# A state-space layer and a soft mixture of experts on one core: TensorE's due sums move between the halves of its long pieces

## The chip, the cores and the metric

The program runs on one NeuronCore of one Trainium2 chip. The metric is the time of one execution on the device in microseconds (us); the lower the better. TensorE is called PE here, VectorE DVE, ScalarE ACT, GpSimd POOL and SyncE SP, as in the profile.

## The reference, cut to what matters

The input x has 16 sequences of 512 positions and 256 channels. First comes a bidirectional state-space layer: a projection to 512 inner channels, a causal convolution of width 4, then for each of two directions, each of the 512 channels and each of 16 states a running sum over the positions:

```
dA_cum = exp(reverse cumulative sum of dt * A[d, n])
xs     = cumsum(dt * u * B[n] * dA_cum) / (dA_cum + 1e-12)
y      = sum over n of xs[n] * C[n]  +  u * D
```

The result is gated and projected back to 256 channels, and `x = layernorm(x + layer(x))`. Then comes a soft mixture of 16 experts with 64 slots each over groups of 1024 positions (two sequences):

```
logits   = layernorm(x) . slot embeddings          (1024 positions x 1024 slots)
slots    = softmax over positions (logits)^T . x   (dispatch)
eout     = (gelu(slots Wg + bg) * (slots Wu + bu)) Wd + bd,  for each expert
out      = softmax over slots (logits) . eout      (combine)
```

and again `x = layernorm(x + experts(x))`. All data are float32.

## The kernel before

A sequence is called a batch b in the code (b = 0 to 15). For each batch `scan_part` runs four times: two directions r and two halves p of the channels, a half having two chunks c of 128 channels. It loops over pairs of states n and over the two chunks, so there are 8 x 2 steps in a part and 1024 steps in all. One step does this:

- ACT makes two exponentials `h` (L420) and two tanh `th` (L422);
- POOL makes `db` = dt*u*B for the two states (L403);
- DVE runs two scans (L426 forward, L428 backward) and two products `hg` (L431); the tile `hg` has four buffers (`bufs=4`);
- POOL multiplies `hg` by C for both states (L432);
- PE sums `hg` over the states into a PSUM tile `acc` by eight transposes (L347). This is the sum that the change moves. For the first states of a part a term u*D follows (L360), and at the very first a matmul with zeros opens the tile (L343).

The sum isn't issued in the step that makes its product. The step appends it to `pending`, and `add_up(depth)` issues the oldest sums until no more than `depth` are left; the step calls `add_up(2)` as the last thing, so a sum is issued two steps after its product was. In states 5 and 13 the product with B is made by PE instead of POOL (`by_diagonal`, tile `hd`, L381), at the step's start.

All other work is cut into pieces and given out beside the scan. A piece is the code of a generator between two `yield`s, and there are three queues of generators (class `Side`): `prep` for the projections of the next part, `front` for the end of a batch (`finish`, `dispatch`) and `back` for experts and combine. `beside_scan` takes up what was left open (evictions of PSUM by ACT or DVE, after `yield HOLD`) and then gives out at most one piece of each queue. Two pieces lie in a step where their turn and the number of free PSUM banks (three, `bank`) allow it. The end of a step reads:

```
                    beside_scan()
                    if k == 1:
                        diags.pop(0)
                    add_up(2)
```

In PE's order a step is therefore: `hd` where there is one, a piece of `prep`, of `front`, of `back`, and the sum.

The pieces of `back` are these. For each pair of experts: both gate matmuls `pg` (L801 for the bias, L806), both up-projections `pu` (L755, function `up`), both down-projections into one bank `peo` (L782, function `down`). ACT evicts `pg` by Gelu into `ht` (L823 the first, L826 the second), DVE multiplies `ht` by `pu` (L767) and makes `eo` of `peo` (L843). For each 128 positions of combine: both halves of the logits `cl` (L860), evicted by DVE's maxima (L868, L869) and ACT's exponentials `cm` (L874), then transposes `ctp` (L881) and the product with the experts' outputs `cpo` (L938). `front` has transposes `pyt` (L598), the output projection `po` (L609, added to x by DVE at L618), dispatch logits `pl` (L663, evicted by DVE's maximum `nm` at L668 and ACT's `et` at L674 and L676), transposes `pd` (L680, evicted to `dis` at L685) and slots `pq` (L695, evicted to `sl` at L705). `prep` has `pin`, `pres`, `px`, `pz` and `pdu`, among them DVE's `rr` (L313).

The experts of two batches are a group. Group g runs beside the scans of batch 2g + 3 (and 2g + 4 has the combines), so the first experts start with batch 3. The eighth group runs after the last scan, from 5160 us on, with wider buffers.

Weights are loaded by SP (`prefetch`, L736) into three buffers (tag `W`), in the order gate, gate, up, up, down, down. SP also loads B and C of each step (L392, L393).

A framework puts the traced instructions into each engine's queue. `late(...)` pins an instruction behind everything traced before it on its engine; `add_up` does so with the first transpose of a sum.

Of the kernel before, what the change touches and what calls it, by code (L numbers as in the profile page):

```python
# [53 lines left out]
def seq_layers(tc, ident, neghalf, a, out):  # L54
# [22 lines left out]
    with ExitStack() as ctx:  # L77
# [27 lines left out]
        def bank(name):  # L105
            count[0] += 1
            if tail and count[0] % 8 >= 3:
                return tail[0].tile([P, 512], F32, tag="tps", name=name)
            return ps.tile([P, 512], F32, tag="mps", name=name)
# [54 lines left out]
        def late(ins):  # L164

            return tc.keep_in_program_order(ins)
# [549 lines left out]
        def experts(g, lo, hi):  # L716

            b0, rows = 2 * g, 2 * SL
            needs = []
            for ep in range(lo, hi):  # L720
                e0 = 2 * ep
                needs += [("Wg", e0), ("Wg", e0 + 1)]
                needs += [("Wu", e0), ("Wu", e0 + 1), ("Wd", e0), ("Wd", e0 + 1)]
            got, used = {}, [0]

            def prefetch():
                while len(got) < min(used[0] + (AHEAD if wide else 3), len(needs)):
                    key, e = needs[len(got)]
                    if wide:
                        t = wide[0].tile([P, 4 * DM], F32, tag="tW", name=f"{key}_{g}_{e}", bufs=AHEAD)  # L730
                    else:
                        t = p2.tile([P, 4 * DM], F32, tag="W", name=f"{key}_{g}_{e}", bufs=3)
                    src = a[key][e]
                    k = src.shape[0] // P
                    t = t.rearrange("p (k f) -> p k f", k=k)
                    nc.sync.dma_start(t, src.rearrange("(k p) f -> p k f", p=P))  # L736
                    got[key, e] = t

            def load_slots(ep):
                st = p1.tile([P, NM, 2, 2 * SL], F32, tag="st", name=f"st_{g}_{ep}")  # L740
                for k in range(NM):
                    nc.sync.dma_start(
                        st[:, k, :, :],
                        s_dram[b0 : b0 + 2, k, :, ep * 2 * SL : (ep + 1) * 2 * SL].rearrange("b p s -> p b s"),
                    )
                return st

            prefetch()
            st = load_slots(lo)
            yield 0  # L750
            def up(e, j, st):
                pu = bank(f"pu_{g}_{e}")
                for fc in range(NF):
                    for k in range(NM):
                        nc.tensor.matmul(  # L755
                            pu[:, fc * P : (fc + 1) * P],
                            got["Wu", e][:, k, fc * P : (fc + 1) * P],
                            st[:, k, :, j * SL : (j + 1) * SL],
                            start=(k == 0),
                            stop=(k == NM - 1),  # L760
                        )
                used[0] += 1
                return pu

            def times(e, ht, pu):
                for fc in range(NF):
                    ins = nc.vector.scalar_tensor_tensor(  # L767
                        ht[:, fc, :],
                        pu[:, fc * P : (fc + 1) * P],
                        biases["bu"][:, e * NF + fc : e * NF + fc + 1],  # L770
                        ht[:, fc, :],
                        ALU.add,
                        ALU.mult,
                    )
                    if fc == 0:
                        late(ins)

            def down(e0, hts):
                po = bank(f"peo_{g}_{e0}")
                for j, ht in enumerate(hts):  # L780
                    for fc in range(NF):
                        nc.tensor.matmul(  # L782
                            po[:, j * DM : (j + 1) * DM],
                            ht[:, fc, :],
                            got["Wd", e0 + j][:, fc, :],
                            start=(fc == 0),
                            stop=(fc == NF - 1),
                        )
                used[0] += 2
                return po  # L790

            for ep in range(lo, hi):
                e0 = 2 * ep
                yield 2
                pgs = []
                for j in range(2):
                    e = e0 + j
                    pg = bank(f"pg_{g}_{e}")

                    own = ident[: NE * NF, e * NF : (e + 1) * NF].unsqueeze(2).to_broadcast([NE * NF, NF, P])  # L800
                    nc.tensor.matmul(  # L801
                        pg.rearrange("p (f s) -> p f s", f=NF), biases["bg"], own, start=True, stop=False
                    )
                    for fc in range(NF):
                        for k in range(NM):
                            nc.tensor.matmul(  # L806
                                pg[:, fc * P : (fc + 1) * P],
                                got["Wg", e][:, k, fc * P : (fc + 1) * P],
                                st[:, k, :, j * SL : (j + 1) * SL],
                                start=False,  # L810
                                stop=(fc == NF - 1 and k == NM - 1),
                            )
                    pgs.append(pg)
                used[0] += 2
                yield HOLD
                prefetch()
                hts = []
                for j, pg in enumerate(pgs):
                    e = e0 + j
                    ht = p2.tile([P, NF, rows], F32, tag="ht", name=f"ht_{g}_{e}")  # L820
                    args = (ht.rearrange("p f s -> p (f s)"), pg, AF.Gelu)
                    if j == 0:
                        late(nc.scalar.activation(*args))  # L823
                    else:
                        with tc.high_priority():
                            nc.scalar.activation(*args)  # L826
                    hts.append(ht)
                yield GAP + 2
                pus = [up(e0 + j, j, st) for j in range(2)]
                if ep + 1 < hi:  # L830
                    st = load_slots(ep + 1)
                bd = p2.tile([P, 2, DM], F32, tag="bd", name=f"bd_{g}_{e0}", bufs=1)
                nc.sync.dma_start(bd, a["bd"][e0 : e0 + 2, :].unsqueeze(0).to_broadcast([P, 2, DM]))
                yield HOLD
                prefetch()
                for j in range(2):
                    times(e0 + j, hts[j], pus[j])
                yield GAP + 1
                po = down(e0, hts)
                yield HOLD  # L840
                prefetch()
                eo = p2.tile([P, 2, DM], F32, tag="eo", name=f"eo_{g}_{e0}", bufs=1)
                late(nc.vector.tensor_tensor(eo.rearrange("p e o -> p (e o)"), po, bd.rearrange("p e o -> p (e o)"), ALU.add))  # L843
                nc.sync.dma_start(e_dram[e0 : e0 + 2, b0 * SL : (b0 + 2) * SL, :].rearrange("e s o -> s e o"), eo)
# [6 lines left out]
        def weights(b, lc, x2, keep):  # L851
# [3 lines left out]
            t = x2.pop()  # L855
            cls = []
            for h in range(2):
                cl = bank(f"cl_{i}_{h}")
                for k in range(NM):
                    nc.tensor.matmul(  # L860
                        cl, t[:, k, :], seT[:, k, h * 512 : (h + 1) * 512], start=(k == 0), stop=(k == NM - 1)
                    )
                cls.append(cl)
# [34 lines left out]
        def all_weights(b, kept):  # L898
            x2 = [load_x2(b, 0)]
            yield 0  # L900
            for lc in range(NL):
                kept[b, lc] = yield from weights(b, lc, x2, True)
# [111 lines left out]
        back.add(1, all_weights(2 * g, kept))  # L1014
        side_by_side()
        front.add(1, experts(g, 0, 8))
        back.add(1, all_weights(2 * g + 1, kept))
        side_by_side()
# [49 lines left out]
```

## Time and profile before

| | before |
|---|---|
| median of 3 runs | 5432.52 us (5432.14 to 5433.58) |
| the profiled execution, its own time | 5434.84 us |
| its span, first to last instruction | 5432.9 us |
| mean granted clock of TensorE | 0.89 of full speed |
| instructions in the span | 73685 |
| data moved by DMA | 907.73 MB, 167 GB/s on the mean |

A row of a group gives line, engine, operation, what is written and read, the shapes and the number of instructions, then the busy time and the mean of one in ns, then the time that the engine sat idle just before these instructions and what ended most of that. The waits give for each line the instruction that it waited for, the total in us, how often and the longest. Float32 matmuls that aren't transposes show as two records each. PEld stands for TensorE's weight loads, which overlap its matmuls.

### The profile page before, as it was taken

What the parts mean: (1) busy time and instruction counts of PE and PEld (TensorE: products, weight loads), DVE (VectorE), ACT (ScalarE), POOL (GpSimd) and SP (SyncE); (2) the same over time, 40 slices, a digit from 0 to 9 for tenths busy, and PEclk for the clock granted to TensorE, in tenths of its full rate; (3) what the DMA queues carried; (4) which work ended last, traced back from release to release, by engine and by line L of the source; (5) the groups of instructions that cost most, each with busy time, mean ns of one, the idle gap of its engine ahead of it and who ended that gap; (6) DMA issues with size and microseconds to landing.
All of it is one profiled execution on the core that took longest, in us unless ns stands there. A gap on an engine that the chain in (4) does not pass through costs nothing. (4 is left out here: it accounts for less than half of the span.)

```text
span 5432.9 us, 73685 instructions
## 1 busy us (share of the span) xinstructions
PE 4336.3 (80%) x24145; PEld 3393.4 (62%) x24145; DVE 4552.0 (84%) x6276; ACT 4091.6 (75%) x6517; POOL 4732.3 (87%) x2537
## 2 busy tenths in 40 slices
PE   4656666898878977788788978889777887878889
PEld 3545555676667765677656766667656775667657
DVE  6888989889888898888988988988989889887722
ACT  6677777887788777887878887788778887777641
POOL 6999999999999899998999989998999989988600
PEclk7677878898889989899889988899888998989999
DMA  4333434575446754566446754467444774457435
GB/s 129 130 122 132 130 124 131 192 231 161 151 141 212 228 148 145 157 220 213 134 137 195 230 173 150 130 215 231 151 145 143 226 224 132 144 178 234 126 104 184
DMA packets 595237, 907.73 MB, mean 167 GB/s; under 512 B 78083, under 2 KB 384899, under 8 KB 594853
## 3 DMA queue, kind: packets, MB, share of 16 engines
q1 hardware_dynamic: 521156, 859.87, 49.9%
q10 hardware_dynamic: 73696, 43.14, 2.8%
q8 instruction: 192, 3.15, 0.2%
q14 instruction: 193, 1.57, 0.1%
HBM read 840.86 MB, written 62.01 MB: 166 GB/s over the span
## 5 line engine op out<-in xcount | busy, mean ns | idle before, releaser
L432 POOL TENSOR_TENSOR hg<-hg,cs 128x1024 f32<-128x1024 f32 x1024 | 2415.3, 2362 | 129.7 <-DVE hg L431 111.4
L403 POOL TENSOR_TENSOR db<-du,bs 128x1024 f32<-128x1024 f32 (+1 forms) x1024 | 2138.8, 2092 | 240.4 <-DVE h L426 93.5
L347 PE MATMUL acc<-ident,hg 128*128 128x128 f32 x8192 | 1191.7, 296 | 207.3 <-POOL hg L432 183.2
L431 DVE SCALAR_TENSOR_TENSOR hg<-th,h 128x512 f32<-128x512 f32 x1792 | 1186.2, 678 | 188.8 <-PE acc L347 110.4
L347 PEld LDWEIGHTS acc<-ident,hg 128*128 128x128 f32 x8192 | 1053.5, 155 | 399.4 <-POOL hg L432 251.0
L426 DVE TENSOR_TENSOR_SCAN h<-h,db 128x512 f32<-128x512 f32 x896 | 1071.3, 1218 | 97.5 <-ACT h L420 92.0
L428 DVE TENSOR_TENSOR_SCAN h<-h,db 128x512 f32<-128x512 f32 x896 | 1072.1, 1218 | 96.1 <-ACT h L420 92.9
L422 ACT ACTIVATE th<-rr,Ah_f 128x512 f32<-128x512 f32 x1024 | 724.5, 714 | 189.2 <-DVE hg L431 187.7
L422 ACT ACTIVATE th<-rr,Ah_b 128x512 f32<-128x512 f32 x1024 | 721.6, 712 | 166.1 <-DVE hg L431 151.3
L420 ACT ACTIVATE h<-dt,A_f 128x512 f32<-128x512 f32 x896 | 608.0, 681 | 115.2 <-DVE hg L431 112.1
L420 ACT ACTIVATE h<-dt,A_b 128x512 f32<-128x512 f32 x896 | 608.6, 681 | 105.0 <-DVE hg L431 102.9
L663 PE MATMUL pl<-x2T,seT 128*128 128x512 f32 x512 | 286.0, 687 | 73.6 <-DVE hg L431 36.2
L381 PE MATMUL hd<-dg,duT 128*128 128x128 f32 x2048 | 309.0, 300 | 35.3 <-ACT yt L603 15.2
L806 PEld LDWEIGHTS pg<-st,Wg 128*128 128x128 f32 x2048 | 245.4, 196 | 107.8 <-issue 85.4
L381 PEld LDWEIGHTS hd<-dg,duT 128*128 128x128 f32 x2048 | 286.1, 216 | 41.8 <-ACT yt L603 17.8
L938 PE MATMUL cpo<-ceo,ct 128*128 128x256 f32 x1024 | 266.3, 420 | 48.5 <-DVE rr L313 38.8
L782 PE MATMUL peo<-Wd,ht 128*128 128x256 f32 x1024 | 253.5, 403 | 48.2 <-DVE rr L313 30.5
L755 PE MATMUL pu<-st,Wu 128*128 128x128 f32 x2048 | 252.3, 282 | 44.6 <-DMA Wu<-in_Wu_dram 18.6
L755 PEld LDWEIGHTS pu<-st,Wu 128*128 128x128 f32 x2048 | 242.6, 196 | 55.8 <-DVE h L428 17.6
L938 PEld LDWEIGHTS cpo<-ceo,ct 128*128 128x128 f32 x1024 | 214.0, 213 | 99.6 <-DVE rr L313 44.0
L806 PE MATMUL pg<-st,Wg 128*128 128x128 f32 x2048 | 270.3, 287 | 5.6 <-DMA Wg<-in_Wg_dram 3.6
L860 PE MATMUL cl<-seT,cx 128*128 128x512 f32 x512 | 251.3, 631 | 29.1 <-ACT et L674 18.2
(151 smaller groups left out, 6621.3 us busy)
## 6 DMA issues: line engine op xcount, KB each, us to landing
cs<-bc SPq DMA_DIRECT2D x512, 512.0 KB, 4.0
bs<-bc SPq DMA_DIRECT2D x384, 512.0 KB, 5.0
Wg<-in_Wg_dram SPq DMA_DIRECT2D x128, 512.0 KB, 6.1
Wu<-in_Wu_dram SPq DMA_DIRECT2D x128, 512.0 KB, 5.7
Wd<-in_Wd_dram SPq DMA_DIRECT2D x128, 512.0 KB, 5.5
dg<-diag_dram SPq DMA_DIRECT2D x128, 256.0 KB, 4.4
bs<-bc SPq DMA_DIRECT2D x128, 256.0 KB, 3.6
x<-in_x_dram SPq DMA_DIRECT2D x32, 512.0 KB, 6.6
```

What stands on the lines that cost most here:

```text
L347: ins = nc.tensor.matmul(accs[c][:, s], hc[:, j, s], ident, is_transpose=True, start=False, stop=(last and j == 1 and lc == NL - 1),)
L381: ins = nc.tensor.matmul(h[:, s], v[c][3][:, s], dg[:, s], start=True, stop=True)
L403: nc.gpsimd.tensor_tensor(db[:, :k, :], du.unsqueeze(1).to_broadcast([P, k, L]), bs[:, :k, :], ALU.mult)
L420: nc.scalar.activation(hs[j][1], dt, AF.Exp, scale=w["A"][:, c, s])
L422: nc.scalar.activation(ths[j], rr, AF.Tanh, bias=LN_1E12 / 2, scale=w["Ah"][:, c, s])
L426: nc.vector.tensor_tensor_scan(h, dec, add, 0.0, ALU.mult, ALU.add)
L428: nc.vector.tensor_tensor_scan(h[:, ::-1], dec[:, ::-1], add[:, ::-1], 0.0, ALU.mult, ALU.add)
L431: nc.vector.scalar_tensor_tensor(hg[:, j, :], th, 1.0, h, ALU.add, ALU.mult)
L432: nc.gpsimd.tensor_tensor(hg, hg, cs, ALU.mult)
L755: nc.tensor.matmul(pu[:, fc * P : (fc + 1) * P], got["Wu", e][:, k, fc * P : (fc + 1) * P], st[:, k, :, j * SL : (j + 1) * SL], start=(k = ...
L806: nc.tensor.matmul(pg[:, fc * P : (fc + 1) * P], got["Wg", e][:, k, fc * P : (fc + 1) * P], st[:, k, :, j * SL : (j + 1) * SL], start=Fals ...
L938: nc.tensor.matmul(po[:, :DM], cts[sc // 4][:, sc % 4 * P : (sc % 4 + 1) * P], eos[sc // 4][:, sc % 4, :], start=(sc == 0), stop=(sc == NS ...
```

## The change

A call of `add_up(2)` is put between the two halves of the long pieces that have two halves: between the gate matmuls of a pair, between the up-projections, between the two halves of the down-projection, and between the two halves of the combine logits. The call at the end of each step stays.

```
             def down(e0, hts):
                 po = bank(f"peo_{g}_{e0}")
                 for j, ht in enumerate(hts):
+                    if j:
+                        add_up(2)
                     for fc in range(NF):
                         nc.tensor.matmul(
...
                 pgs = []
                 for j in range(2):
+                    if j:
+                        add_up(2)
                     e = e0 + j
                     pg = bank(f"pg_{g}_{e}")
...
                 yield GAP + 2
-                pus = [up(e0 + j, j, st) for j in range(2)]
+                pus = [up(e0, 0, st)]
+                add_up(2)
+                pus.append(up(e0 + 1, 1, st))
                 if ep + 1 < hi:
                     st = load_slots(ep + 1)
...
             for h in range(2):
+                if h:
+                    add_up(2)
                 cl = bank(f"cl_{i}_{h}")
                 for k in range(NM):
                     nc.tensor.matmul(
```

More of the change, by code (lines that the diff above doesn't have):

```diff
@@ L780, in down @@
                 for j, ht in enumerate(hts):
+                    if j:
+                        add_up(2)
                     for fc in range(NF):
@@ L796, in experts @@
                 for j in range(2):
+                    if j:
+                        add_up(2)
                     e = e0 + j
@@ L828, in experts @@
                 yield GAP + 2
-                pus = [up(e0 + j, j, st) for j in range(2)]
+                pus = [up(e0, 0, st)]
+                add_up(2)
+                pus.append(up(e0 + 1, 1, st))
                 if ep + 1 < hi:
@@ L857, in weights @@
             for h in range(2):
+                if h:
+                    add_up(2)
                 cl = bank(f"cl_{i}_{h}")
```

## Prediction

> **What bounds the kernel now.** I read the page first (busy time, groups), then who waited for whom, then the timeline around the places that the change touches.
>
> ```profile
> PE 4336.3 (80%) x24145; PEld 3393.4 (62%) x24145; DVE 4552.0 (84%) x6276; ACT 4091.6 (75%) x6517; POOL 4732.3 (87%) x2537
> ...
> L432 POOL TENSOR_TENSOR hg<-hg,cs 128x1024 f32<-128x1024 f32 x1024 | 2415.3, 2362 | 129.7 <-DVE hg L431 111.4
> L347 PE MATMUL acc<-ident,hg 128*128 128x128 f32 x8192 | 1191.7, 296 | 207.3 <-POOL hg L432 183.2
> ```
>
> POOL is the busiest, but only the stretch before expert work starts runs at its pace: from 300 to 900 us POOL is busy 582 of 600 us. Between 900 and 4800 us POOL is busy 3612 of 3900 us, VectorE (DVE) 3461, TensorE (PE) 3218, ScalarE (ACT) 3121. No engine is full; the time is set by a chain that hops between all four. The change acts there, so what counts is where that chain passes through PE.
>
> ```profile
> DVE hg L431 <- PE acc L347: 110.4, 82, 4.8
> DVE hd L428 <- PE hd L381: 74.0, 48, 9.0
> DVE nm L668 <- PE pl L663: 62.0, 37, 9.2
> DVE ht L767 <- PE pu L755: 56.8, 18, 12.7
> DVE eo L843 <- PE peo L782: 49.0, 19, 5.3
> ```
>
> (Total us, times, longest.) The first row is what the change aims at: DVE wants to write a state product into one of four `hg` buffers, and the sum that reads it (PE, L347) isn't done. The other rows are the counterweight: DVE waits for PE's pieces too, and whatever is put ahead of the end of a piece makes these longer.
>
> **What the Trainium skill says.** "PSUM — Partial Sum Buffer", section "Engine vs sequencer instructions": matmuls start and complete in program order, and the other engines' queues are strict FIFO. So a sum put before a second half delays that half by its whole length, and the reader's engine stands. The trace agrees: in each step PE's records come piece, then sum. "TensorE: Matmul & The Clock Gate", section "What's actually happening": after an idle window TensorE's clock is halved until it was busy again for some us. The trace agrees: half an up-projection takes 1.95 us within a run and 3.75 us after 3.98 us of idleness, and the sum behind it 1.92 instead of 1.04 us.
>
> **The change, part by part.** It adds and removes no instruction and no DMA. `pending` holds three sums at most while pieces are given out, so each inserted `add_up(2)` can give out one sum at most, and the one at the step's end then does nothing. In the last part (after 5160 us) `pending` is empty. Matched against the order on PE, 221 of 1024 sums move: 56 each behind first gates, ups and downs, 53 behind first combine logits. Of each step only the order on PE changes: half, sum, half instead of half, half, sum.
>
> *Wait added.* PE's second half now stands behind the wait of the sum for POOL's product (L432). In all 221 places that product ended before the first half did, by 0.4 us or more. Cost nothing, cover: those 0.4 us; bounds 0 and +5 us.
>
> *Price of a move.* 8 transposes, 1.04 us from first start to last end, 1.0 us net on a running PE, since records overlap (1.9 us for 13 sums with the direct term L360 or a slow clock). The sum ends earlier by the second half and whatever lay between (2 to 3 us), the second half ends 1.0 us later, and PE's work behind both is where it was, unless PE idled before the second half (buffer or DMA wait). That is so in 39 places, and the sum goes into the idle time: 36.6 us in all, most of it off the chain.
>
> *Queues moved past.* None on SP or POOL. The weight buffer of a second half is freed 1.0 us later and its next load (5.5 to 6.1 us to landing) starts later. The one such wait that recurs on the chain, `Wu` at 2362, is issued when SP gets past a `cs` load that waits for POOL, so I take 0; bounds 0 and +1 us for each of 7 expert groups.
>
> *Gains by the naive count.* 49 of DVE's waits on a sum, 61.7 us, are behind sums that move. But look at what ends the next wait:
>
> ```profile
> 2460.53 1.04 PE L347 MATMUL acc<-ident,hg 128*128 128x128 f32 x8
> ...
> 2461.41 1.06 PE L381 MATMUL hd<-dg,duT 128*128 128x128 f32 x8
> 2461.61 0.69 DVE L431 SCALAR_TENSOR_TENSOR hg<-th,h 128x512 f32<-128x512 f32 x1 [1.72 <-PE acc L347]
> ...
> 2462.50 1.23 DVE L426 TENSOR_TENSOR_SCAN hd<-dec,hd 128x512 f32<-128x512 f32 x1 [0.20 <-PE hd L381]
> ```
>
> Start, duration, and in brackets the idle time and its releaser. With the sum before the second gate the 1.72 us go, but the next scan needs `hd`, which PE delivers at 2462.46 in either order, so its 0.20 become 1.9 us. PE works without a gap from 2442 to 2472, so an exchange inside that run helps nobody who waits for the run's later products. The same holds for the waits of 2.3 us at 2304 (then DVE stands for `po`, L618) and at 2527 (then for ACT, next line).
>
> *Losses.* The same kind of place seen from the other side:
>
> ```profile
> 2378.04 0.69 DVE L843 TENSOR_TENSOR eo<-peo,bd 128x512 f32<-128x512 f32 x1
> ...
> 2432.76 0.69 DVE L668 TENSOR_REDUCE nm<-pl 128x1 f32<-128x512 f32 x1 [0.40 <-PE pl L663]
> 2433.49 0.69 ACT L674 ACTIVATE et<-pl,nm 128x512 f32<-128x512 f32 x1 [2.56 <-DVE nm L668]
> ...
> 2526.91 1.04 PE L347 MATMUL acc<-ident,hg 128*128 128x128 f32 x8
> 2527.11 0.60 ACT L826 ACTIVATE ht<-pg 128x512 f32<-128x512 f32 x1 [0.30 <-PE pg L806]
> 2527.72 1.28 ACT L420 ACT_TABLE_LOAD   x1
> ```
>
> The second gate's Gelu (L826) starts 0.04 us after the gate ends (2527.07), and ACT's table load and the exponentials that DVE wants stand behind it: +1.0 us. So does the down-projection's `eo` (2378.04, 0.03 us after `peo` ends), and `nm` of the dispatch logits `pl`, which lie between a second half and the sum, with `et` waiting behind it.
>
> *The sum.* The page's own chain starts at 5084 us, so I followed it on by the same rule, by hand, from 5160 back to 60 us: where an instruction was preceded by idleness, go to its releaser, else to the one before it on its engine. The pattern repeats from expert group to expert group (batches 3, 5, ..., 15). Where the chain leaves PE:
> - for `eo` 11 times, one of them behind a 2.50 us DMA wait that takes the sum in: 10 x 1.0;
> - for the second Gelu 6 times: 6.0; for `nm` behind a delayed `pl` 6 times: 6.0; for slots `pq` behind a second gate once: 1.0;
> - in batch 15 three sums with 0.18 us waits, whose DVE predecessor (`eo`, `nm`) gets late: 2.6. Together +25.6 us.
> - For a sum that moves with a real wait: 6 times, behind the second up-projection that waits for `Wu` (0.51, 0.97, 1.19, 1.04, 0.57, 0.65): -4.9 us. There the sum goes into the DMA wait.
> - 6 times a sum that lay behind `pd` on the chain is now before the second up-projection: -0.4 each, -2.4. Three more sums in DMA or buffer waits of batch 15: -2.4. Together -9.7 us.
> - 4 times for combine logits `cl`, each behind a 3.36 us buffer wait that takes the sum in: 0.
>
> Net +15.9 us. A delay on the chain adds in full; a gain lasts only until the next chain takes over, so the true number is hardly below that by this route, unless the order of the other engines changes. The profiled execution has 5434.84 us (span 5432.9 and 1.9 around it), so 5450.7; the median shown is 2.3 us lower, so **5448 us**.
>
> **Rivals.**
> - *Freed buffers decide (faster).* If DVE keeps what it gains because PE, relieved in 39 places, runs ahead of its consumers, the 61.7 us go and the 31 second halves whose readers already stand waiting cost 1.0 us each: -31, 5402 us. For it: POOL waits 111.4 us for DVE's `hg`. Against: the `hd` wait above. It decides where more than half of the 49 waits aren't followed by another wait for PE within some 5 us; of the 7 in the group from 2255 to 2560 us I found 2 like that.
> - *Exchange without effect.* PE's unbroken runs take in both the gains and the losses: within 10 us of 5432. For it: total work and order of products at the end of a run are the same. Against: the Gelu and `eo` readers have no slack.
> - *Other order elsewhere.* Only some instructions are pinned to program order; the build may place others on DVE or ACT anew once sums sit elsewhere. Up to 30 us either way; nothing in the trace prices it.
> - *No change at all:* were `pending` at two, nothing would move. The order on PE (one sum at the end of every step) excludes that.
>
> **Numbers.** A measurement of this kernel tells about 0.2% (10.9 us) from no change. Forecast 55% (45 slower, 10 within), its own range 5438 to 5464; freed buffers 27% (25 faster, 2 within); no effect 18% (14 within, 2 each side). Faster 0.27, same 0.26, slower 0.47. The range 5410 to 5464 leaves out about 14% below (the stronger half of the freed buffers) and 6% above (bounds of the weight loads, another order).
>
> **What would show it.** Right: the row DVE `hg` on PE `acc` falls from 110 to some 55 us, while `eo` on `peo`, `ht` L826 on `pg` and `nm` on `pl` rise, each by 10 us or more in the scan, and `hd` on PE `hd` rises by 15 or more; POOL's waits for DVE don't fall. Wrong: `hd` doesn't rise and POOL's `hg <- DVE hg` falls by 20 us or more (freed buffers), or the order on DVE and ACT differs.

## The result, and the profile after

| | before | after |
|---|---|---|
| median | 5432.33 us (4 runs, 5424.75 to 5433.58) | 5481.24 us (4 runs, 5479.35 to 5493.22) |
| the profiled execution, its own time | 5434.84 us | 5493.22 us |
| its span | 5432.9 us | 5491.3 us |
| mean granted clock of TensorE | 0.89 | 0.88 |

The ratio is 1.0096 [1.0081, 1.0111]: 49 us slower at the medians. The forecast was 5448 us, 16 us slower; the loss is three times that. The profiled execution after is 12 us above its median, so a few us of its rows are its own. From the page of the kernel after, the busy times and POOL's largest group:

```profile
PE 4380.7 (80%) x24143; PEld 3422.0 (62%) x24145; DVE 4544.9 (83%) x6276; ACT 4141.5 (75%) x6549; POOL 4734.5 (86%) x2537
...
L432 POOL TENSOR_TENSOR hg<-hg,cs 128x1024 f32<-128x1024 f32 x1024 | 2418.4, 2365 | 142.5 <-DVE hg L431 107.3
```

The striking number is ACT's count: 6549 instructions where there were 6517, and 50 us more busy time. The edit touches no ACT instruction. The waits of the kernel after (total us, times, longest):

```profile
DVE h L428 <- ACT h L420: 128.9, 74, 7.0
DVE h L426 <- ACT h L420: 115.3, 53, 7.8
...
DVE hg L431 <- PE acc L347: 83.4, 44, 6.4
...
DVE eo L849 <- PE peo L784: 55.3, 15, 6.3
...
DVE nm L668 <- PE pl L663: 54.0, 27, 9.3
```

DVE's wait for the sums falls by 27 us (110.4 to 83.4). The waits that were to rise by 10 us or more don't: `eo` +6, `nm` -8, ACT's wait for the second gate -4 (23.9 to 19.6). POOL's wait for DVE stays, as forecast (111.4 to 107.3). DVE's waits for ACT's exponentials `h`, which the prediction's list of rows doesn't have, rise from 184.9 us (92.9 and 92.0) to 244.2. So much of the lost time shows as waiting for ACT. Its groups say what the 32 instructions are; the first block is of the kernel before, the second of the kernel after (lines below L780 are shifted there: L823, L826 are L827, L830).

```profile
L420 ACT ACT_TABLE_LOAD x121 | 155.2, 1283 | 2.2
...
L826 ACT ACT_TABLE_LOAD x23 | 29.5, 1283 | 0.4
```

```profile
L420 ACT ACT_TABLE_LOAD x132 | 169.4, 1283 | 2.2
...
L830 ACT ACT_TABLE_LOAD x42 | 53.9, 1283 | 0.7
```

Gelu and the exponential need different tables of function values, and where one follows the other on ACT, a table load (ACT_TABLE_LOAD) stands between them. It is put down to the line of the instruction that needs it. Before, 41 of the 64 second Gelus (L826) found their table still in place, because the first Gelu (L823) stood right ahead of them or only a tanh lay between; after, only 22 do. In 19 more pairs an exponential now stands between the two Gelus. In 13 of them that makes two loads more, for the second Gelu and for the next exponential; in the six that are the last pair of a group it makes one more, as the function behind (L296) needed a load before too. By lines it is +19 at L830, +11 at L420, +7 at L674 and -5 at L422: +32 loads of 1.283 us, 41 us of the 50. The trace agrees with the Trainium skill, "ScalarE: Activation LUTs", section "What ACT_TABLE_LOAD costs", on the load itself (some 1283 ns); the drain of some 1380 ns that the page adds to it does not show here, as the timeline below has no gap around a load.

Where do the exponentials come from? Compared instruction by instruction, PE's queue differs by the moved sums alone (called the exchange from here on), but the framework also placed 1382 of ACT's 6073 instructions, 1954 of DVE's 6276, 145 of POOL's and 388 of SP's in other places than before. The prediction had this as a rival ("other order elsewhere") and left it at 30 us either way.

### The profile page after: what moved, and what is told of

Its sections match the earlier page's. It is cut to its first block, busy times and chain, and to the rows that moved or that the text cites. A ratio compares the mean times of both kernels' runs of the same rounds, so it can differ in the third digit from the quotient of the medians.

```text
span 5491.3 us, 73662 instructions
## 1 busy us (share of the span) xinstructions
PE 4380.7 (80%) x24143; PEld 3422.0 (62%) x24145; DVE 4544.9 (83%) x6276; ACT 4141.5 (75%) x6549; POOL 4734.5 (86%) x2537
## 4 chain that ended last, share of the span: by engine, by line
DVE 36%; PE 23%; ACT 19%; issue 11%; POOL 5%; DMA 2%; DVEq 0%; SPq 0%; ACTq 0%; POOLq 0%
DVE h L428 9%; DVE h L426 9%; DVE hg L431 8%; PE acc L347 4%; ACT h L420 4%; ACT th L422 4%; POOL hg L432 2%; POOL db L403 2%; PE cpo L946 2%; ACT L420 2%; PE pq L695 2%; PE pg L810 2%; PE pl L663 2%; PE hd L381 1%; PE peo L784 1%
## 5 line engine op out<-in xcount | busy, mean ns | idle before, releaser
L432 POOL TENSOR_TENSOR hg<-hg,cs 128x1024 f32<-128x1024 f32 x1024 | 2418.4, 2365 | 142.5 <-DVE hg L431 107.3
L347 PE MATMUL acc<-ident,hg 128*128 128x128 f32 x8192 | 1208.5, 298 | 209.0 <-POOL hg L432 187.9
L347 PEld LDWEIGHTS acc<-ident,hg 128*128 128x128 f32 x8192 | 1067.6, 156 | 404.7 <-POOL hg L432 252.0
L431 DVE SCALAR_TENSOR_TENSOR hg<-th,h 128x512 f32<-128x512 f32 x1792 | 1185.8, 677 | 161.3 <-PE acc L347 83.4
L422 ACT ACTIVATE th<-rr,Ah_f 128x512 f32<-128x512 f32 x1024 | 724.7, 713 | 195.2 <-DVE hg L431 193.2
L422 ACT ACTIVATE th<-rr,Ah_b 128x512 f32<-128x512 f32 x1024 | 722.7, 712 | 129.9 <-DVE hg L431 112.7
L420 ACT ACTIVATE h<-dt,A_b 128x512 f32<-128x512 f32 x896 | 608.1, 680 | 123.1 <-DVE hg L431 120.2
L420 ACT ACTIVATE h<-dt,A_f 128x512 f32<-128x512 f32 x896 | 609.2, 681 | 117.9 <-DVE hg L431 115.2
L946 PE MATMUL cpo<-ceo,ct 128*128 128x256 f32 x1024 | 252.2, 404 | 45.2 <-DVE rr L313 40.9
```

Source lines behind the costliest of these rows:

```text
L347: ins = nc.tensor.matmul(accs[c][:, s], hc[:, j, s], ident, is_transpose=True, start=False, stop=(last and j == 1 and lc == NL - 1),)
L420: nc.scalar.activation(hs[j][1], dt, AF.Exp, scale=w["A"][:, c, s])
L422: nc.scalar.activation(ths[j], rr, AF.Tanh, bias=LN_1E12 / 2, scale=w["Ah"][:, c, s])
L431: nc.vector.scalar_tensor_tensor(hg[:, j, :], th, 1.0, h, ALU.add, ALU.mult)
L432: nc.gpsimd.tensor_tensor(hg, hg, cs, ALU.mult)
L946: nc.tensor.matmul(po[:, :DM], cts[sc // 4][:, sc % 4 * P : (sc % 4 + 1) * P], eos[sc // 4][:, sc % 4, :], start=(sc == 0), stop=(sc == NS ...
```

## The experiments

All ratios are to the kernel before, measured beside it on the same chip; a point is one per cent of its time. "Orders held" means this addition, with which a kernel's queue on an engine is the one of another kernel, instruction by instruction (`own` is what was traced for an engine, `at` the order to keep); no instruction is added:

```
+def in_order(tc):
+    for key, code in _ORDER.items():
...
+        for before, after in zip(at, at[1:]):
+            tc.add_manual_dep(
+                own[after],
+                own[before].name,
+                mybir.DependencyInfo(mybir.DependencyClass.NoSync, mybir.DependencyReason.DATA),
...
         seq_postln_kernel(tc, args, out)
+        in_order(tc)
```

**The exchange alone, and the other orders alone.** First, PE in the changed order and ACT, DVE, POOL and SP held to the queues of before:

> PE's queue in the order of the changed kernel, the queues of ACT, DVE, POOL and SP held to the order of the kernel before. Theory (the exchange on PE costs what the chain said, the rest of the 49 us came from new orders elsewhere, ACT's 32 more table loads above all): 342 table loads, ratio to before 1.001 to 1.005, about 5448 us. Rival 1 (the exchange on PE alone costs it all, the chain count was too low): 1.008 to 1.011, about 5480. Rival 2 (the exchange is free or a gain): at or below 1.000.

Measured 5441.82 us, 1.0006 [0.9998, 1.0014], a little under the theory. Second, PE in the order of before and the other four held to the queues of after:

> PE's queue in the order of the kernel before, the queues of ACT, DVE, POOL and SP held to the order that the changed kernel has. Theory (new orders elsewhere): 374 table loads, 5460 to 5475 us, ratio 1.005 to 1.008. Rival 1 (the exchange on PE alone): ratio 0.999 to 1.002. If both parts only cost together, each of this run and of the run with PE's order alone is near 1.000.

Measured 5589.76 us, 1.0276 [1.0262, 1.0290], far above every forecast. So in the old queues the exchange costs 3 us, between -1 and +8, and the loss comes only with the other queues. The two parts don't add up: in the new queues the earlier sums are needed, and without them the time is another 1.8 points higher. The waits of the kernel with the exchange alone:

```profile
DVE hd L428 <- PE hd L381: 73.2, 45, 8.5
DVE nm L668 <- PE pl L663: 72.0, 42, 7.6
DVE hg L431 <- PE acc L347: 68.3, 33, 4.4
...
DVE eo L849 <- PE peo L784: 61.7, 37, 6.0
...
DVE hd L426 <- PE hd L381: 46.4, 33, 4.5
```

With only PE's order changed, most of the predicted shifts are there: `hg` on `acc` falls by 42 us, `nm` rises by 10, `eo` by 13, `hd` by 13 (both rows). Only the time doesn't follow.

**Which queue.** PE has the changed order in all five of these. What isn't held is placed by the framework.

> The changed kernel with ACT's queue alone held to the order of the kernel before; DVE, POOL and SP as the framework places them then. Theory (ACT's table loads are the hidden part): 342 loads and the time of the run with PE's order alone, ratio 1.001 to 1.005. Rival (DVE's or SP's new order is what costs): stays at 1.007 to 1.011.

(The change with only ACT held to before's queue.) Measured 5480.10 us, 1.0075 [1.0061, 1.0089], with 342 loads: as the rival said, a loss without one more table load.

> The changed kernel with DVE's queue alone held to the order of the kernel before; ACT's is placed by the framework and has 374 table loads (32 more), SP's and POOL's are placed by it too. Theory A (ACT's table loads cost): 1.004 to 1.007. Theory B (DVE's new order costs, the loads lie in ACT's idle time): 0.999 to 1.003. Theory C (SP's order of loads costs): 1.005 to 1.009.

(The change with only DVE held.) Measured 5506.75 us, 1.0128 [1.0114, 1.0142], with 374 loads: above all three forecasts.

> The changed kernel with ACT's and DVE's queues held to the order of before, SP's and POOL's free (SP differs from before in 205 of 2188 places, POOL in 18). Theories A and B: 1.000 to 1.002, as with PE's order alone. Theory C (SP): 1.005 or more.

(Both held.) Measured 5446.73 us, 1.0018 [1.0012, 1.0025].

> The changed kernel with SP's and POOL's queues held to the order of before, ACT's and DVE's as in the changed kernel (374 loads). Theories A and B: 1.008 to 1.011, the whole loss. Theory C (SP's order): 1.000 to 1.003.

(SP and POOL held to before's, ACT and DVE to after's.) Measured 5486.82 us, 1.0090 [1.0075, 1.0105].

> PE's and SP's queues in the order of the changed kernel, ACT, DVE and POOL in the order of before. Theories A and B: 1.000 to 1.003. Theory C (SP's order): 1.006 to 1.010, nearly the whole loss.

(All held to before's but SP, which has after's.) Measured 5454.49 us, 1.0035 [1.0022, 1.0047], between the two forecasts.

The first two of these runs can't be read as "only DVE new" and "only ACT new". With one queue held, the framework placed the others anew: compared in the traces by operation, line and tiles, DVE's queue in the first run differs from before's in 925 places and from after's in 1480 (before's and after's differ in 1685 by this count), and ACT's in the second run in 762 and 1578. They show that other orders of DVE, SP and POOL can cost 0.75% without a table load more, and that yet another order of ACT, with 32 loads more and SP and POOL placed anew, can cost 1.28%. The other three are firmer: ACT's and DVE's new orders together, with SP and POOL held, make 0.90 of the 0.96 points; with both old 0.18 is left; SP's new order alone costs 0.35, but hardly shows beside those two (1.0090 with SP and POOL held, 1.0096 without). After's order of ACT alone, or of DVE alone, with all others old wasn't tried.

**Which of the four places.** Edits of the change alone, nothing held:

> The change made between the two gate matmuls alone; downs, ups and combine logits as before. It has 374 table loads by its queue (32 more than before, all of the change's). Theory (table loads): most of the loss, ratio 1.005 to 1.008 (32 loads of 1.28 us are 41 us of ACT, and 6 delayed Gelus on the chain 6 us). Rival (every piece's second half costs alike): a quarter of the 49 us, 1.002 to 1.003.

```
                 for j in range(2):
+                    if j:
+                        add_up(2)
                     e = e0 + j
```

Measured 5478.31 us, 1.0070 [1.0057, 1.0083]; 374 loads, and the pairs that it splits are the same 19.

> The change between downs, ups and combine logits, but not between the gates: 322 table loads, 20 fewer than before. Theory A: 0.993 to 1.000. Theory B: 1.003 to 1.008, since DVE's queue differs from before in 1549 of 6276 places.

(The change without these two lines.) Measured 5454.56 us, 1.0034 [1.0022, 1.0046]; 322 loads.

> The change made between the two halves of the downs alone: 322 table loads, 20 fewer than before; DVE's queue differs from before in 418 places. Theory A: 0.994 to 0.999. Theory B: 1.000 to 1.003. If the delayed eo cost what the chain count said (10 x 1.0 us on PE's order): 2 us above these.

(The two lines in `down` alone.) Measured 5439.76 us, 1.0010 [1.0003, 1.0017]; 322 loads.

The sum between the gates brings the 32 loads and most of the loss. That it puts the second gate later in the framework's plan, so that an exponential is ready before its Gelu, fits this, but I did not look into the plan. The last two have 20 loads fewer than before and are slower all the same, `only_downs` by little, as their theories B said: the count of loads alone doesn't set the time.

**Adjacent Gelus by the source.** The second gate's Gelu is queued first and the first one's right behind it:

```
-                hts = []
-                for j, pg in enumerate(pgs):
-                    e = e0 + j
+                hts = [None, None]
+                for j in (1, 0):
+                    e, pg = e0 + j, pgs[j]
...
-                    if j == 0:
+                    if j == 1:
                         late(nc.scalar.activation(*args))
...
-                    hts.append(ht)
+                    hts[j] = ht
```

> The changed kernel, with the Gelu of the second gate queued on ACT first and that of the first gate behind it, so that both share one table: 295 table loads instead of 374, 79 x 1.28 = 101 us less on ACT. Theory A (table loads carry the loss): 0.985 to 0.996 of before. Theory B (a bad match of the orders on ACT and DVE, loads aside): 1.004 to 1.012, as the orders stay scrambled.

(On the kernel after.) Measured 5399.02 us, 0.9934 [0.9921, 0.9946].

> The kernel before with the two Gelus adjacent in the same way: 295 table loads instead of 342, 47 x 1.28 = 60 us less on ACT. Theory A: 0.987 to 0.995, and within 0.3% of the changed kernel with adjacent Gelus. Theory B: 0.997 to 1.005, and 0.5% or more faster than the changed kernel with adjacent Gelus.

(On the kernel before.) Measured 5373.57 us, 0.9887 [0.9873, 0.9900]: the best version found, faster than both kernels. Both have 295 loads. I took the 1.13% for the price of 47 loads, 1.3 us each. But the two kernels with adjacent Gelus lie 0.5 points apart, as theory B had it, and DVE's queue changed in 810 places too, so loads and orders were still mixed.

**Loads and orders told apart.** Four kernels with all queues held, in which one thing differs.

> PE in the changed order; DVE, POOL and SP in the order of before; ACT in the order of before except that in the 19 pairs whose Gelus the changed kernel splits, the second Gelu stands behind the next exponential (52 of 6073 places differ): 374 table loads instead of 342. Theory L (the split Gelus and their loads are the loss): 32 loads at the 1.33 us that a load was worth in the kernels with adjacent Gelus, some 43 us, so 1.006 to 1.010. Theory O (the orders apart from the loads are the loss): 0.999 to 1.003, as with the order on PE alone (1.0006).

Measured 5487.54 us, 1.0093 [1.0078, 1.0108]. Moving 19 Gelus on ACT behind the next exponential, and nothing else, makes a loss of nearly the whole size: 0.87 points over the exchange alone, some 47 us.

> The changed kernel with all orders as they are in it, except that on ACT the 19 second Gelus stand ahead of the exponential again (50 of 6073 places differ): 342 table loads instead of 374. Theory L: 1.000 to 1.004. Theory O: 1.007 to 1.010, like the changed kernel (1.0096). In between, both count.

Measured 5467.33 us, 1.0059 [1.0046, 1.0072]. In the new queues the same 19 Gelus are worth 0.37 points; 0.59% stays. So the split is one cause and the new orders apart from it are another, and they overlap: 0.87 and 0.53 points over the exchange alone are more than the whole loss, so part of what the split costs in the old queues is lost in the new ones anyway.

> PE in the changed order; DVE, POOL and SP in the order of before; ACT in the order of before except that in 30 pairs the first Gelu is moved back to stand next to the second: 301 loads instead of 342. Theory L: 41 loads at 1.33 us, some 54 us less, 0.989 to 0.993. Theory O: 0.997 to 1.002; above 1.003 if DVE's products, which now get the first Gelu later, stand for it.

Measured 5433.14 us, 0.9992 [0.9983, 1.0000]. 41 loads fewer than with the exchange alone bring 0.14 points, about what the two intervals leave uncertain, and not the 1 point that theory L gave. So a load has no fixed price. The places differ: the 19 pairs of `split_gelus` are the fourth, sixth and eighth of the first six groups and one of the seventh, while those that had loads to lose here are mostly the first three of a group.

> The kernel adjacent_gelus_before with the changed order on PE and its own orders on ACT, DVE, POOL and SP held (295 loads). If the exchange on PE costs nothing by itself: 0.987 to 0.990, as without it (0.9887), and the 0.5% between the two kernels with adjacent Gelus is the orders of the others. If the exchange costs something once the loads are gone: 0.992 to 0.995 (like adjacent_gelus, 0.9934).

Measured 5370.57 us, 0.9887 [0.9871, 0.9903]: the exchange costs nothing there either, and the 0.5% between the two kernels with adjacent Gelus is the other queues.

**What a split does.** The same place in the timelines of the kernel with the exchange alone and of `split_gelus`, at the fourth pair of a group; just ahead of it the second is 11.4 us behind. First the exchange alone (start, duration, instruction, idle time and its releaser):

```profile
2394.36 0.60 ACT L827 ACTIVATE ht<-pg 128x512 f32<-128x512 f32 x1
...
2394.86 0.59 ACT L830 ACTIVATE ht<-pg 128x512 f32<-128x512 f32 x1
...
2395.01 1.14 PE L326 MATMUL pdu<-ident,du 128*128 128x128 f32 x8 [0.38 <-ACT ht L827]
...
2395.99 1.04 PE L347 MATMUL acc<-ident,hg 128*128 128x128 f32 x8
```

Then `split_gelus`:

```profile
2405.74 0.60 ACT L827 ACTIVATE ht<-pg 128x512 f32<-128x512 f32 x1
...
2406.39 0.66 PE L326 MATMUL pdu<-ident,du 128*128 128x128 f32 x4 [0.38 <-ACT ht L827]
2406.96 1.28 ACT L420 ACT_TABLE_LOAD   x1
...
2408.26 0.69 ACT L420 ACTIVATE h<-dt,A_f 128x512 f32<-128x512 f32 x1
2408.97 1.28 ACT L830 ACT_TABLE_LOAD   x1
...
2410.26 0.60 ACT L830 ACTIVATE ht<-pg 128x512 f32<-128x512 f32 x1
...
2410.91 1.12 PE L326 MATMUL pdu<-ident,du 128*128 128x128 f32 x4 [3.87 <-ACT ht L830]
...
2411.82 1.91 PE L347 MATMUL acc<-ident,hg 128*128 128x128 f32 x8
...
2412.05 0.69 DVE L431 SCALAR_TENSOR_TENSOR hg<-th,h 128x512 f32<-128x512 f32 x1 [1.77 <-PE pdu L326]
...
2413.99 1.23 DVE L426 TENSOR_TENSOR_SCAN h<-h,db 128x512 f32<-128x512 f32 x1 [1.26 <-ACT h L420]
```

Two things follow from the split here. A Gelu empties a PSUM bank, and four of the eight transposes `pdu` go into the bank that the second Gelu empties; with an exponential and two loads ahead of it that is 4.0 us later against the first Gelu (4.52 us between the starts of the two Gelus instead of 0.50). PE stands for 3.87 us, and the sum behind `pdu` takes 1.91 us instead of 1.04, at a granted clock of 0.50. Beside that, ACT itself has two loads more to do, 2.6 us, in a stretch in which it is never idle, and the exponential that DVE's next scan reads (it starts at 2413.27, and at 2399.09 with the exchange alone) comes 2.8 us later.

The last line shows which of the two sets the time here: the scan waits for the exponential (L420), and would have started no earlier had PE not stood. The product ahead of it (2412.05) is put down to the end of the transposes (2412.03), but the tanh that it reads ended at 2411.96. DVE's `res` (L989), two instructions behind that scan, starts at 2402.06 and 2415.93: 13.87 us apart, 2.5 more than ahead of the split, which is about the two loads. All six groups show the same at the fourth pair, and at the sixth DVE's scan waits 1.6 to 1.9 us for the exponential, again behind an unbroken stretch of ACT.

The eighth pair is the other way round. The exchange alone, then `split_gelus`:

```profile
2533.82 1.91 PE L347 MATMUL acc<-ident,hg 128*128 128x128 f32 x16
```

```profile
2551.90 0.66 PE L680 MATMUL pd<-ident,et 128*128 128x128 f32 x4 [1.59 <-ACT ht L830]
...
2552.39 3.37 PE L347 MATMUL acc<-ident,hg 128*128 128x128 f32 x16
...
2554.09 0.69 DVE L431 SCALAR_TENSOR_TENSOR hg<-th,h 128x512 f32<-128x512 f32 x1 [2.89 <-PE acc L347]
```

Here the transposes `pd` stand 1.59 us for the bank of the second Gelu, the two sums behind them take 3.37 us instead of 1.91 (granted clock 0.54 instead of 1.00), and DVE waits for them: it falls 2.8 to 3.3 us behind at this place in each of the six groups, right after a gain of 1.1 us, as the exponential now comes ahead of the Gelu. PE's waits of `split_gelus` show both places, six times each; in the kernel with the exchange alone neither row occurs:

```profile
PE pdu L326 <- ACT ht L830: 23.2, 6, 3.9
PE pd L680 <- ACT ht L830: 9.5, 6, 1.6
```

And of the kernel after, where the change itself made the splits:

```profile
PE pdu L326 <- ACT ht L830: 21.5, 6, 3.8
PE pd L680 <- ACT ht L830: 10.6, 6, 1.8
```

In `after_rejoined` both rows are gone. Taken at the first Gelu of each pair of experts, `split_gelus` falls behind the exchange alone group by group: 1.0 us at the first pair of the first group, then 7.5, 12.3, 19.7, 26.8, 34.9 and 42.2 us at that of the next six. From the second group on 2.8 to 3.0 us of each step come between the fourth pair and the fifth, and 1.6 to 2.0 between the sixth and the seventh. No run separates ACT's own delay from that of the banks; that the first decides at the fourth and sixth pairs and the second at the eighth is read from what ended DVE's waits.

In `joined_gelus` the saving meets other waits. ACT, without an exponential and its loads between the two, comes to the second Gelu before its gate is done, and what DVE no longer waits for ACT it waits for PE:

```profile
L830 ACT ACTIVATE ht<-pg 128x512 f32<-128x512 f32 x64 | 38.1, 595 | 42.9 <-PE pg L810 42.9
```

```profile
DVE h L428 <- ACT h L420: 100.3, 73, 7.1
DVE h L426 <- ACT h L420: 81.5, 38, 6.0
DVE eo L849 <- PE peo L784: 75.3, 36, 5.7
```

ACT stands 42.9 us for these gates, 24.6 with the exchange alone: 18 of the 53 us of loads go there. DVE's waits for the exponentials fall by 29 us (211.0 to 181.8), but those for `peo` rise by 14 (61.7 to 75.3) and those of L618 for the output projection `po` by 9 (21.0 to 29.6).

## Why the prediction was right or wrong

**The change of PE's order: right.** Four kinds of pieces, one sum given out between the halves, nothing else on PE.

**Wait added at no cost: right.** With the exchange alone PE waits 181.5 us for POOL's products (L432) ahead of the sums, as against 183.2 before.

**The sum of the chain (+25.6, -9.7, net +15.9): too high.** In the old queues it measured 3 us, between -1 and +8. The counts for `eo` (10) and `nm` (6) came as waits of +13 and +10 us, but "a delay on the chain adds in full" failed: DVE's wait for `acc` fell by 42 us and POOL's for `hg` by 25 (111.4 to 86.1), and gains and losses nearly cancel. The six delayed Gelus didn't come: ACT's wait for the second gate is 24.6 us, as against 23.9. So with the exchange alone "POOL's waits for DVE don't fall" failed too; this much of the rival "freed buffers" is true, without its gain. The rival "exchange without effect" describes the exchange on PE best.

**The naive gains (61.7 us) come back as other waits: right in the main.** With the exchange alone `hg` on `acc` fell to 68 us, where 55 were forecast, and `hd` rose by 13, where 15 or more were.

**"Unless the order of the other engines changes": this is where the loss is.** The step that failed is the term for the other order: the 5448 us put it at nothing, and the rival at "up to 30 us either way; nothing in the trace prices it". It was 46 us (the 49 less the 3 of the exchange). That the kernel got slower, as forecast, is luck: the chain that was to make it slower hardly did. The trace of before could not price the term, but it did show what was at stake: 23 table loads at L826 for 64 Gelus say that 41 pairs shared one table, and two loads of 1.283 us for each are 105 us of ACT. The prediction saw that the second Gelu gets later (it charged 1 us for it), not that ACT's queue could be filled between the two.

**What stays open.** Of the 0.96%, the split alone makes 0.87 points in the old queues but only 0.37 in the new ones, where the other places cost 0.5 points without it. Which places those are, of DVE's 1954, of SP's 388 or of the rest of ACT's, is not known. Nor is it known why the Gelus made adjacent by the source gain 62 us in the kernel before with 47 loads fewer, while `joined_gelus` gains 8 with 41 fewer.

## What to carry to other kernels

Where a framework places what isn't pinned, an edit on one engine can be an edit on all of them: compare the queues of every engine before costing it, and count the table loads, which show a rearranged ACT at a glance. To price the edit itself, hold the other queues to their old order; here that left 3 us of a loss of 49. Hold all of them at once: with one queue held, the framework placed the others anew. And don't add the parts up: the other orders alone, without the edit, cost 150 us. Keep functions of one table together where ACT has no idle time and another engine waits for what comes next, and ask of each eviction which matmul waits for its bank.

## What the runs showed of the hardware

- A table load has no price of its own. 32 more of them, 41 us of ACT, came with a loss of 47 us where DVE waited for the exponential behind them or PE for a bank (`split_gelus`); 41 fewer, 53 us of ACT, gained 8 us where ACT and DVE then waited for PE (`joined_gelus`).
- Tanh needs no load behind a Gelu nor behind an exponential: in the timeline of the exchange alone, L422 runs at 2395.33, right behind a Gelu, and at 2398.47, behind an exponential and a copy, without a load; the exponential between (2397.37) has one ahead of it. The Trainium skill, "ScalarE: Activation LUTs", section "Table sets: the hidden batching unit", lists tanh in the set of exp; that Gelu's has it too is what this trace shows.
- Idleness of PE can be paid twice. In `split_gelus` the sum behind 3.87 us of it and four transposes took 1.91 us instead of 1.04, at a granted clock of 0.50; behind 1.59 us at the eighth pair two sums took 3.37 us instead of 1.91, at 0.54. Only the second was seen to hold up DVE.
